# The feed-forward part of a batch as units between the next batch's score steps

## The chip, the cores and the metric

The kernel runs on one core of a Trainium2 chip. Its five engines work at the same time and wait for each other by semaphores: TensorE (PE) multiplies, VectorE (DVE) and ScalarE (ACT) work on tiles in SBUF and PSUM, GpSimd (POOL) works on tiles in SBUF, and SyncE (SP) issues most of the DMAs. The metric is the device time of one execution in microseconds.

## The reference

The input x is 4 batches of 1024 rows of 256 values. A memory of 77 rows per batch stands ahead of the keys. There are two blocks, each with a residual:

```
y  = x + attention(layernorm(x), mem)       16 heads of 16, causal behind the 77 memory rows, output projection and bias
out = y + ffn(layernorm(y))
ffn(v) = quant(gelu(quant(v) @ quant(w_fc).T + b_fc)) @ quant(w_proj).T + b_proj
```

`quant` gives each block of 32 values along a row one exponent, from the largest magnitude of the block, and rounds to 3 bits of mantissa. The hidden width is 1024, Gelu is the exact one.

## The kernel before, in words

A tile is 128 rows; there are 32 tiles, 8 in a batch. The heads are worked on in groups of four, so there are 16 head groups `kk`, four to a batch. A head group takes 14 steps of two half-steps (`half_step`, L662). In a half-step PE makes two pieces of score rows for the next group, from which DVE takes row maxima (`max_matmul` L400, `max_reduce` L423 and L425), and two pieces of transposed scores for this group (`score_matmul`, L463), which ACT turns into exponentials (`score_exp`, L474) and POOL masks (L479). `times_v` (L500) multiplies them with the values, two steps later. Row maxima go through DRAM back into a row of q (`put_max`, L436 and L437). After half of a group's steps `pack` copies the sums (L522) and sends them by DMA into `o_pk` and, the row sums, into DRAM.

PSUM has two buffers for the transposed scores (`ps_st`), three small ones that all else shares (`ps_s`, through `s_tile`), and one for the sums (`ps_av`).

The order of the work is written out: every engine runs its instructions in the order in which this program issues them (`manual_schedule`). `run` (L680) puts other work, called units, between half-steps. A unit is a function or a list of stages; `begin` runs the first at once and the others three half-steps apart (`LATER`), `tick` runs what is due. Before, the units of a head group are spread by their number. Units are the statistics and the normalization of the next batch (`stats_unit`, `norm_unit`), its projections (`v_unit`, `qk_unit`, `move_unit`), the quantized weights of the feed-forward part during batch 0 (`weight_unit`), the division by the row sums (`divide_unit`: a DMA in, a reciprocal on DVE L549, a DMA out, 16 broadcasting DMAs L557, two products on POOL L566) and the output projection with the first residual (`wout_unit`, L578 to L584).

All of x lies in SBUF from the start (`x_all`, loaded at L82); the residual is added into it. When attention is done for all batches, `inv_std` makes 32 inverse deviations at once, and a loop over the 32 tiles runs the feed-forward part with pools of its own: `in_unit` (normalize L781, quantize L188 to L201, transpose L788), `hid_unit` one tile behind it (matmuls L798 and L801, Gelu L806, quantize), `out_unit` two tiles behind (transpose L814, copy L816, matmuls L819 and L820, residual L822, output L823).

```
    for t in range(TT + 2):
        if t < TT:
            in_unit(t)
        if 1 <= t <= TT:
            hid_unit(t - 1)
        if t >= 2:
            out_unit(t - 2)
```

Of the kernel before, what the change touches and what calls it, by code (L numbers as in the profile page):

```python
# [17 lines left out]
P = 128  # L18
# [25 lines left out]
def kernel(  # L44
# [34 lines left out]
    x_all = const.tile([P, TT, D], F32, name="x_all")  # L79

    def load_x(t0, n):
        nc.sync.dma_start(  # L82
            out=x_all[:, t0 : t0 + n, :],
            in_=xf[t0 * P : (t0 + n) * P, :].rearrange("(t p) d -> p t d", p=P),
        )

    for t0 in range(0, NT, 2):
        load_x(t0, 2)
    ctx_sb = const.tile([M, B, D], F32, name="ctx_sb")
    nc.scalar.dma_start(out=ctx_sb, in_=mem.rearrange("b m d -> m b d"))  # L90
# [6 lines left out]
    for b in range(1, B):  # L97
        for half in range(2):
            load_x(b * NT + half * NT // 2, NT // 2)

# [58 lines left out]
    def stats(t, mv):  # L159
        st = small.tile([P, 6], F32, name="st")  # L160
        nc.vector.bn_stats(st, x_all[:, t, :])
        nc.vector.bn_aggr(mv[:, t, :], st)
# [18 lines left out]
    def block_quant(pool, src, n, dst):  # L181
# [4 lines left out]
        src3 = src.rearrange("p (n k) -> p n k", k=QBLK)  # L186
        amax = small.tile([P, nb], F32, name=f"amax{n}")
        nc.vector.tensor_reduce(amax, src3, axis=AX.X, op=ALU.max, apply_absolute_value=True)  # L188
        mag = small.tile([P, nb], F32, name=f"mag{n}")
# [7 lines left out]
        magb = mag.unsqueeze(2).broadcast_to([P, nb, QBLK])  # L197
        up = pool.tile([P, n], F32, name=f"up{n}")
        up3 = up.rearrange("p (n k) -> p n k", k=QBLK)
        nc.vector.tensor_tensor(up3, src3, magb, ALU.add)  # L200
        nc.gpsimd.tensor_tensor(  # L201
            dst.rearrange("p (n k) -> p n k", k=QBLK), up3, magb, ALU.subtract
# [9 lines left out]
    with ExitStack() as actx:  # L212
        ap = lambda name, bufs, **kw: actx.enter_context(tc.tile_pool(name=name, bufs=bufs, **kw))
        keep = ap("keep", 1)
        xtp = ap("xtp", 2)
        osp = ap("osp", 3)
        opp = ap("opp", 3)
        rbp = ap("rbp", 1)
        dram = ap("dram", 2, space=bass.MemoryType.DRAM)
        work = ap("work", 3)  # L220
        ptp = ap("ptp", 7)
        wst = ap("wst", 2)
# [17 lines left out]
        q_st = keep.tile([P, N], F32, name="q_st")  # L240
        k_st = keep.tile([P, KEYS], F32, name="k_st")
# [28 lines left out]
        normed = {b: 0 for b in range(B)}  # L270

        def stats_unit(b, half):
            def emit():
# [3 lines left out]
                if half == 1:  # L277
                    inv_std(mv1, rstd1, b * NT, (b + 1) * NT)
# [584 lines left out]
```

## Time and profile before

| | |
|---|---|
| time, median of 3 runs | 1213.57 us (1187.82 to 1215.45) |
| profiled execution | 1219.08 us, its span 1217.3 us |
| mean granted TensorE clock | 0.846 |
| busy: PE, DVE, ACT, POOL | 92%, 63%, 41%, 20% |
| tables loaded on ACT | 2 |
| last copy of attention sums (L522) | 981.1 us |

The profile is of one execution; the figures below come from it. A line of a group gives the source line, engine, operation, output and inputs with their shapes, the count, the busy time and the mean of one in ns, and then how long the engine stood before them and what ended that. A line of waits gives who waited for whom, the total in us, how often, and the longest. PE's busy time is modelled: a busy PE isn't PE at its peak. The clock line shows in tenths what clock the array was granted in each fortieth of the span.

### The profile page before, as it was taken

How to read it: one execution, taken by the hardware profiler on the slowest of the kernel's cores; microseconds unless marked ns; L12 is line 12 of the kernel's file. 1: busy time of each engine (PE TensorE's matmuls, PEld its weight loads, DVE VectorE, ACT ScalarE, POOL GpSimd, SP SyncE). 2: the span in 40 equal slices, each digit the busy share in tenths (PEclk: the TensorE clock that was granted, in tenths of full speed). 3: DMA queues.
4: the chain of work that ended last, by engine and by line, in shares of the span. 5: the costliest groups of instructions: out<-in, count | busy, mean ns of one | idle time of the engine just before them, and what ended most of it. 6: DMA issues, size and time to landing. Idle time of an engine off the chain costs nothing. (4 is left out here: it accounts for less than half of the span.)

```text
span 1217.3 us, 21139 instructions
## 1 busy us (share of the span) xinstructions
PE 1115.3 (92%) x8024; PEld 451.3 (37%) x8024; DVE 763.8 (63%) x2176; ACT 497.4 (41%) x708; POOL 247.1 (20%) x435
## 2 busy tenths in 40 slices
PE   3998999999979999997999999999999966888996
PEld 2433333433324334432343443434333232443333
DVE  7765765657557675665576665667772028997765
ACT  2123444534423555442435455444554302443333
POOL 3010211021111110112011110222111023445342
PEclk9976789979959999997799999999997565775557
DMA  7000001000110011003000100110000100000000
GB/s 218 22 20 15 19 20 35 24 19 21 38 49 2 12 26 25 8 8 76 11 6 16 40 3 12 44 44 7 6 12 7 25 25 0 31 23 22 22 18 27
DMA packets 31383, 32.17 MB, mean 26 GB/s; under 512 B 13364, under 2 KB 24942, under 8 KB 31281
## 3 DMA queue, kind: packets, MB, share of 16 engines
q1 hardware_dynamic: 29856, 29.43, 9.0%
q8 instruction: 63, 1.03, 0.4%
q10 hardware_dynamic: 1425, 1.38, 0.4%
q14 instruction: 39, 0.32, 0.1%
HBM read 12.39 MB, written 5.24 MB: 14 GB/s over the span
## 5 line engine op out<-in xcount | busy, mean ns | idle before, releaser
L474 ACT ACTIVATE pt<-st_ps 128x1024 f32<-128x1024 f32 (+4 forms) x448 | 354.1, 793 | 452.3 <-PE st_ps L463 236.3
L400 PE MATMUL s_ps<-kT,qT 32*128 32x205 f32 (+3 forms) x1736 | 498.2, 552 | 29.3 <-DVE mxp L425 19.2
L463 PE MATMUL st_ps<-qT,kT 32*128 32x512 f32 (+5 forms) x1792 | 513.1, 576 | 1.1 <-ACT pt L474 0.7
L425 DVE CUSTOM_DVE_ANT_0 junk<-s_ps,tri,mx 128x293 bf16<-128x293 f32 (+3 forms) x372 | 228.4, 614 | 91.6 <-PE s_ps L400 54.1
L400 PEld LDWEIGHTS s_ps<-kT,qT 32*128 32x128 f32 x1736 | 200.5, 195 | 210.6 <-issue 93.9
L479 POOL TENSOR_SCALAR_AFFINE_SELECT pt<-pt 128x254 f32<-128x254 f32 (+3 forms) x320 | 117.4, 367 | 772.0 <-ACT pt L474 772.0
L500 PE MATMUL av_ps<-pt,vaug 128*32 128x256 f32 (+7 forms) x3072 | 237.9, 384 | 6.0 <-POOL pt L479 3.6
L423 DVE TENSOR_REDUCE mx<-s_ps 128x1 f32<-128x296 f32 (+3 forms) x310 | 159.3, 554 | 97.6 <-PE s_ps L400 74.9
L463 PEld LDWEIGHTS st_ps<-qT,kT 32*128 32x128 f32 (+1 forms) x1792 | 199.3, 196 | 21.8 <-ACT pt L474 10.5
L500 PEld LDWEIGHTS av_ps<-pt,vaug 128*32 128x32 f32 (+1 forms) x3072 | 63.1, 112 | 267.6 <-issue 203.7
L425 DVE CUSTOM_DVE_ANT_0 junk<-s_ps,tri 128x205 bf16<-128x205 f32 (+2 forms) x186 | 94.2, 507 | 88.1 <-PE s_ps L400 62.4
L201 POOL TENSOR_TENSOR hq<-up,mag 128x1024 bf16<-128x1024 f32 x32 | 61.4, 1918 | 56.5 <-DVE up L200 50.5
L819 PE MATMUL y_ps<-wprT,hT 128*128 128x256 bf16 x256 | 51.1, 366 | 15.6 <-ACT hT L816 15.6
L798 PE MATMUL h_ps<-wfcT,xqT 128*128 128x512 bf16 x128 | 58.3, 536 | 2.8 <-ACT xqT L790 2.6
L578 PE MATMUL s_ps<-wo_sb,o_pk 128*128 128x256 f32 x128 | 42.0, 453 | 12.3 <-POOL o_pk L566 11.5
L806 ACT ACTIVATE h<-h_ps 128x1024 f32<-128x1024 f32 x32 | 32.8, 1025 | 48.3 <-PE h_ps L801 31.2
L549 DVE RECIPROCAL r<-sm 128x64 f32<-128x64 f32 x8 | 4.4, 550 | 76.6 <-DMA sm<-sums 76.6
L816 ACT COPY hT<-ht_ps 128x1024 bf16<-128x1024 bf16 x32 | 32.4, 1012 | 43.2 <-PE ht_ps L814 43.0
L188 DVE TENSOR_REDUCE amax<-h 128x32 f32<-128x1024 f32 x32 | 38.8, 1214 | 16.0 <-ACT h L806 15.9
L819 PEld LDWEIGHTS <-hT 128*128 128x128 bf16 x256 | 30.6, 127 | 32.6 <-ACT hT L816 19.2
L319 PE MATMUL s_ps<-wv,xT 128*128 128x256 f32 (+1 forms) x144 | 42.4, 419 | 0.1
L425 DVE DVE_READ_ACCUMULATOR2_ANT mxp<- 128x1 f32 x512 | 42.2, 82 | 0.0
(87 smaller groups left out, 783.9 us busy)
## 6 DMA issues: line engine op xcount, KB each, us to landing
kT<-k_st SPq DMA_DIRECT2D x16, 275.2 KB
qT<-q_st SPq DMA_DIRECT2D x16, 256.0 KB
o_pk<-o_st SPq DMA_DIRECT2D x32, 128.0 KB
rb<-rd SPq DMA_DIRECT2D x128, 32.0 KB
out_dram<-y_sb SPq DMA_DIRECT2D x32, 128.0 KB
x_all<-in_x_dram SPq DMA_DIRECT2D x6, 512.0 KB
x_all<-in_x_dram SPq DMA_DIRECT2D x4, 256.0 KB
sums<-o_st SPq DMA_DIRECT2D x64, 4.0 KB
```

The source lines that it names most:

```text
L201: nc.gpsimd.tensor_tensor(dst.rearrange("p (n k) -> p n k", k=QBLK), up3, magb, ALU.subtract)
L319: nc.tensor.matmul(vp[:nj, :], xT[b][:, k, jt * P : jt * P + nj], wv[:, k, :], start=(k == 0), stop=(k == KC - 1),)
L400: nc.tensor.matmul(sp[:, 0 : hi - lo], qTs[kk % NQK][rows, it * P : (it + 1) * P], kTs[kk % NQK][rows, lo:hi], start=True, stop=True,)
L423: nc.vector.tensor_reduce(into, sp[:, 0:w], axis=AX.X, op=ALU.max)
L425: nc.vector.tensor_tensor_reduce(junk[:, 0:w], sp[:, 0:w], mask, 1.0, before, ALU.add, ALU.max, into)
L463: nc.tensor.matmul(st[:nj, e, : i1 - i0], kTs[kk % NQK][rows, t * P : t * P + nj], qTs[kk % NQK][rows, i0:i1], start=True, stop=True,)
L474: nc.scalar.activation(pt[:nj, :, :w], st[:nj, :, :w], AF.Exp, scale=scale)
L479: nc.gpsimd.affine_select(out=pt[:nj, :, :behind], in_=pt[:nj, :, :behind], compare_op=ALU.is_ge, fill=0.0, base=base, pattern=[[0, 2], [1 ...
L500: nc.tensor.matmul(acc[c * PAD : (c + 1) * PAD, off + lo : off + hi], vaugs[b % 2][:nj, t, v0 : v0 + PAD], pts[kk, n, c // 2][:nj, c % 2, ...
L578: nc.tensor.matmul(yp, o_pk[b, it * P // ICW][:, k, it * P % ICW : it * P % ICW + P], wo_sb[:, k, :], start=(k == 0), stop=False,)
L798: nc.tensor.matmul(hp[:, cols], src[:, k, :], wfcT[:, k, cols], start=(k == 0), stop=False)
L819: nc.tensor.matmul(yp, hT[:, k, :], wprT[:, k, :], start=(k == 0), stop=False)
```

## The change

The loop at the end and its pools are gone. The feed-forward part is written as units like the others, and the units of batch b - 1 are put into the head groups of batch b. The last batch's run at the end.

- x is no longer held as a whole. Each batch's x is loaded into `xn` for its normalization, and each tile is loaded again into one of ten `x2` buffers when its residual is added (`wout_unit`), where it stays until it is written out.
- `divide_unit` issues its broadcasting DMAs two per half-step, its two products run on DVE and in two stages, the reciprocal comes four half-steps after the fetch, and both divisions of a batch begin as soon as the sums are there (`urgent`).
- The quantization is split: `quant_steps` finds the rounding constant, `quant_round` adds it in place on DVE and takes it off on POOL.
- `hidden_unit` takes four tiles at a time, in the buffers of the transposed scores, with Gelu on ACT; in the last batch one tile at a time.
- `out_unit` has four stages: `largest`, `rounding` one half-step later, `turn`, `project`.
- A unit has a cost in us and may have a condition (`ready`); `run` spreads units by cost.
- q and k share one staging tile `qk_st`; `pt` has 6 buffers for 7, `o_st` 2 for 3, `xT` 1 for 2, `xh` 4 for 3. The memory rows are loaded per batch.

```diff
...
         nc.vector.tensor_scalar(
             mag, mag, 1.5 * 2.0 ** -126, 2.0 ** (23 - MBITS), ALU.max, ALU.mult
         )
-        magb = mag.unsqueeze(2).broadcast_to([P, nb, QBLK])
+    def quant_round(src, mag, dst):
+        n = src.shape[-1]
+        magb = mag.unsqueeze(2).broadcast_to([P, n // QBLK, QBLK])
+        src3 = src.rearrange("p (n k) -> p n k", k=QBLK)
+        nc.vector.tensor_tensor(src3, src3, magb, ALU.add)
         nc.gpsimd.tensor_tensor(
-            dst.rearrange("p (n k) -> p n k", k=QBLK), up3, magb, ALU.subtract
+            dst.rearrange("p (n k) -> p n k", k=QBLK), src3, magb, ALU.subtract
         )
     mv1 = const.tile([P, TT, 2], F32, name="mv1")
...
-        xtp = ap("xtp", 2)
-        osp = ap("osp", 3)
+        xtp = ap("xtp", 1)
+        xnp = ap("xnp", 2)
+        osp = ap("osp", 2)
         opp = ap("opp", 3)
         rbp = ap("rbp", 1)
+        X2 = 10
+        xrp = ap("xrp", X2)
+        HBUF = 4
+        hp_ = ap("hp", HBUF)
+        ffn = ap("ffn", 2)
         dram = ap("dram", 2, space=bass.MemoryType.DRAM)
-        work = ap("work", 3)
-        ptp = ap("ptp", 7)
-        wst = ap("wst", 2)
+        work = ap("work", 4)
+        ptp = ap("ptp", 6)
         ps_st = ap("ps_st", 2, space=PSUM)
         ps_av = ap("ps_av", 1, space=PSUM)
         ps_s = ap("ps_s", 3, space=PSUM)
...
         mxps = [keep.tile([P, 2 * HPG * NT // 2], F32, name=f"mxp{i}") for i in range(2)]
         for i in range(2):
             nc.gpsimd.memset(mxps[i], 0.0)
...
-            def scale_sums():
-                o = o_pk[b, ic]
-                for k in range(KC):
-                    nc.gpsimd.tensor_tensor(o[:, k, :], o[:, k, :], got["rb"][:, k, :], ALU.mult)
-                divided.add((b, ic))
-            fetch.ready = lambda: sums_of.get((b, ic)) == NG
-            return [fetch, invert, spread, lambda: None, scale_sums]
+                got["rd"] = dram.tile([HEADS, ICW], F32, name="rd")
+                nc.sync.dma_start(out=got["rd"].rearrange("h (s j) -> (h s) j", s=SPH), in_=r)
+                got["rb"] = rbp.tile([P, KC, ICW], F32, name="rb")
+            def spread(h):
+                def emit():
+                    for i in range(h, h + 2):
+                        nc.sync.dma_start(
+                            out=got["rb"][i % HPC * HD : (i % HPC + 1) * HD, i // HPC, :],
+                            in_=got["rd"][i, :].partition_broadcast(HD),
+                        )
+                return emit
+            def scale_sums(k):
+                def emit():
+                    o = o_pk[b, ic][:, k, :]
+                    nc.vector.tensor_mul(o, o, got["rb"][:, k, :])
+                    if k == KC - 1:
+                        divided.add((b, ic))
+                        held["rb"] -= 1
+                return emit
+            fetch.ready = lambda: packed.get((b, ic)) == NG and not held["rb"]
+            stages = [fetch, (4, invert)]
+            stages += [(LATER if h == 0 else 1, spread(h)) for h in range(0, HEADS, 2)]
+            return cost(0.6, stages + [(4, scale_sums(0)), (1, scale_sums(1))])
...
         def wout_unit(b, it):
-            def emit():
-                t = b * NT + it
-                assert (b, it * P // ICW) in divided
+            t = b * NT + it
+            ic = it * P // ICW
+            def fetch():
+                x2[t] = xrp.tile([P, D], F32, name="x2")
+                nc.sync.dma_start(out=x2[t], in_=xf[t * P : (t + 1) * P, :])
...
+                nc.vector.tensor_add(x2[t], x2[t], yp)
+                stats(x2[t], mv2, t)
+                done["wout"] += 1
+            fetch.ready = lambda: (b, ic) in divided and len(x2) - done["out"] < X2
+            return cost(1.8, [fetch, project])
+        def wout_units(b, half):
+            return [wout_unit(b, half * HN + i) for i in range(HN)]
...
+        def root_unit(b, half):
+            def emit():
+                inv_std(mv2, rstd2, b * NT + half * HN, b * NT + (half + 1) * HN)
+                rooted.add(b * NT // HN + half)
+            emit.ready = lambda: done["wout"] >= b * NT + (half + 1) * HN
+            return cost(1.5, emit)
+        def in_unit(t):
+            got = {}
+            def quantize():
+                done["begun"] += 1
+                held["xq"] += 1
+                xh = work.tile([P, D], F32, name="xh")
+                nc.vector.tensor_scalar(
+                    xh, x2[t], mv2[:, t, 0:1], rstd2[:, t : t + 1], ALU.subtract, ALU.mult
+                )
+                got["xq"] = ffn.tile([P, D], BF16, name="xq", bufs=XQ)
+                quant_round(xh, quant_steps(xh, D, "x"), got["xq"])
+            def turn():
+                tp = s_tile([P, KC, P], BF16)
+                for k in range(KC):
+                    nc.tensor.transpose(tp[:, k, :], got["xq"][:, k * P : (k + 1) * P], identb)
+                held["xq"] -= 1
+                xqT[t] = ffn.tile([P, KC, P], BF16, name="xqT", bufs=HBUF + 1)
+                nc.scalar.copy(xqT[t], tp)
+            quantize.ready = lambda: (
+                t // HN in rooted and done["begun"] - len(hs) <= HBUF
+                and held["xq"] < XQ and held["xh"] < XH
+            )
+            return cost(1.6, [quantize, turn])
+        def hidden_unit(tiles):
+            def emit():
+                for t in tiles:
+                    hp = ps_st.tile([P, 2, ICW], F32, name="st_ps")
+                    for n in range(HID // ICW):
+                        for k in range(KC):
+                            nc.tensor.matmul(
+                                hp[:, n, :], xqT[t][:, k, :],
+                                wfcT[:, k, n * ICW : (n + 1) * ICW],
+                                start=(k == 0), stop=False,
+                            )
+                        nc.tensor.matmul(
+                            hp[:, n, :], ones3,
+                            bias3[:, B_FC + n * ICW : B_FC + (n + 1) * ICW],
+                            start=False, stop=True,
+                        )
+                    hs[t] = hp_.tile([P, HID], F32, name="h")
+                    nc.scalar.activation(
+                        hs[t], hp.rearrange("p e n -> p (e n)"), AF.Gelu
+                    )
+            emit.ready = lambda: (
+                all(t in xqT for t in tiles) and len(hs) + len(tiles) - done["round"] <= HBUF
+            )
+            return cost(1.4 * len(tiles), emit)
+        def out_unit(t):
+            got = {}
+            def largest():
+                held["hq"] += 1
+                got["mag"] = quant_steps(hs[t], HID, "h")
+            def rounding():
+                got["hq"] = ffn.tile([P, HID], BF16, name="hq")
+                quant_round(hs[t], got["mag"], got["hq"])
+                done["round"] += 1
+            def turn():
+                tp = s_tile([P, HC, P], BF16)
+                for k in range(HC):
+                    nc.tensor.transpose(tp[:, k, :], got["hq"][:, k * P : (k + 1) * P], identb)
+                held["hq"] -= 1
+                got["hT"] = ffn.tile([P, HC, P], BF16, name="hT")
+                nc.scalar.copy(got["hT"], tp)
+            def project():
+                yp = s_tile([P, D])
+                for k in range(HC):
+                    nc.tensor.matmul(
+                        yp, got["hT"][:, k, :], wprT[:, k, :], start=(k == 0), stop=False
+                    )
+                nc.tensor.matmul(yp, ones3, bias3[:, B_PROJ : B_PROJ + D], start=False, stop=True)
+                nc.vector.tensor_add(x2[t], x2[t], yp)
+                nc.sync.dma_start(out=of[t * P : (t + 1) * P, :], in_=x2[t])
+                done["out"] += 1
+            largest.ready = lambda: t in hs and held["hq"] < 2
+            return cost(4.4, [largest, (1, rounding), turn, project])
...
             stages[0]()
-            for i, stage in enumerate(stages[1:]):
-                pending.append((clock[0] + (i + 1) * LATER, stage))
+            at = clock[0]
+            for stage in stages[1:]:
+                delay, stage = stage if isinstance(stage, tuple) else (LATER, stage)
+                at += delay
+                pending.append((at, stage))
...
-                    share += len(extras) / spots
-                    while (
-                        todo
-                        and len(extras) - len(todo) < share - 1e-6
-                        and ready(todo[0])()
-                    ):
-                        begin(todo.popleft())
+                    share = min(share + rate, 2.5)
+                    if urgent and ready(urgent[0]):
+                        begin(urgent.pop(0))
+                    while todo and share > 0 and ready(todo[0]):
+                        u = todo.popleft()
+                        share -= price(u)
+                        begin(u)
...
+            if g == NG - 1:
+                urgent += [divide_unit(b, 0), divide_unit(b, 1)]
+            if f >= 0:
+                T = range(f * NT, (f + 1) * NT)
                 if g == 0:
-                    extras += batch_units(b + 1) + wouts
-                elif g >= 2:
-                    vs = v_units(b + 1)
-                    extras += vs[:5] if g == 2 else vs[5:]
+                    extras += loads + wout_units(f, 0) + qs + [root_unit(f, 0)]
+                    extras += merge(norms, wout_units(f, 1)) if norms else wout_units(f, 1)
+                    extras += [root_unit(f, 1)]
+                elif g == 1:
+                    extras += [in_unit(t) for t in T[:HN]] + [hidden_unit(T[:HN])]
+                    extras += [out_unit(T[0])] + [in_unit(t) for t in T[HN:]]
+                elif g == 2:
+                    extras += merge(vs[:5], [out_unit(t) for t in T[1:HN]]) + qs
+                    extras += [hidden_unit(T[HN:])]
+                else:
+                    extras += merge(vs[5:], [out_unit(t) for t in T[HN:]])
...
+        T = range((B - 1) * NT, B * NT)
+        todo = urgent + carry
+        chain = lambda ts: [f for t in ts for f in (in_unit(t), hidden_unit([t]), out_unit(t))]
+        todo += merge(chain(T[:HN]), wout_units(B - 1, 1)) + [root_unit(B - 1, 1)]
+        todo += chain(T[HN:])
+        while todo or pending:
             tick()
-        for u in end_units(B - 1):
-            u()
+            for u in list(todo):
+                if getattr(u[0] if isinstance(u, list) else u, "ready", lambda: True)():
+                    todo.remove(u)
+                    begin(u)
+                    break
     mode.close()
-    inv_std(mv2, rstd2, 0, TT)
...
```

## The prediction

> **What bounds the kernel now.** I read the page's busy times and clock first, then stretches by stage, then who waits for whom, then the costliest groups by shape.
>
> ```profile
> PE 1115.3 (92%) x8024; PEld 451.3 (37%) x8024; DVE 763.8 (63%) x2176; ACT 497.4 (41%) x708; POOL 247.1 (20%) x435
> ...
> PEclk9976789979959999997799999999997565775557
> ```
>
> ```profile
> 860.00:880.00 20.00, 20.00 (x204) 7.68 (x201) 15.04 (x45) 9.77 (x13) 3.66 (x10) 1.00 0.01 2
> ...
> 106.00:981.00 875.00, 847.43 (x6801) 330.28 (x6800) 521.93 (x1588) 395.75 (x565) 140.67 (x340) 0.91 0.09 22
> ...
> 981.00:1020.00 39.00, 20.70 (x57) 10.18 (x54) 19.47 (x72) 2.99 (x5) 5.82 (x7) 0.59 0.08 19
> 1020.00:1217.00 197.00, 168.00 (x788) 74.44 (x786) 147.71 (x288) 73.04 (x94) 85.31 (x60) 0.63 0.06 22
> ```
>
> The columns are busy us of PE, PEld, DVE, ACT and POOL, the granted clock, the DMA share, GB/s. There are two stages with different limits. To 981 us the score steps run: PE is named busy nearly throughout, but DVE is at 15.04 of 20 even in a clean stretch. From 981 on comes the tail: the last division and projections, then the feed-forward part (FFN) of all 32 tiles in 197 us, 6.2 us a tile, with half the TensorE clock granted for much of it. The tail is 236 us. So the question is what 24 of the 32 tiles cost when they are put between score steps.
>
> The copies of the attention sums (L522) start at 855.6 and 898.6 us in two consecutive head groups: 43.0 us for 28 half-steps without extras, 1.54 us each. In a half-step DVE reduces twice: the groups of L423 and L425 sum to 529 us over 448 half-steps, 1.18 us each. So about 0.35 us of slack per half-step, with only three PSUM buffers (`ps_s`) between the two engines. PE already waits for DVE's reductions:
>
> ```profile
> PEld s_ps L400 <- DVE mxp L425: 58.3, 92, 5.1
> ...
> PEld s_ps L400 <- DVE mx L423: 31.9, 71, 1.8
> ...
> PE s_ps L400 <- DVE mxp L425: 19.2, 11, 3.9
> ```
>
> What dense DVE work does to the clock is seen where batch 0 quantizes weights (stretches of 4 us, same columns):
>
> ```profile
> 244.00:248.00 4.00, 4.00 (x44) 1.39 (x41) 3.54 (x13) 1.49 (x3) 1.39 (x3) 1.00 0.11 33
> 248.00:252.00 4.00, 3.47 (x30) 1.36 (x26) 3.32 (x13) 0.94 (x3) 1.30 (x3) 0.84 0.12 37
> 252.00:256.00 4.00, 4.00 (x24) 1.44 (x26) 2.44 (x10) 0.67 (x2) 0.88 (x2) 0.50 0.00 0
> 256.00:260.00 4.00, 4.00 (x20) 1.78 (x20) 1.17 (x5) 1.42 (x2) 0.86 (x2) 0.50 0.00 0
> 260.00:264.00 4.00, 4.00 (x21) 1.50 (x20) 1.74 (x9) 2.01 (x3) 0.27 (x1) 0.50 0.00 0
> 264.00:268.00 4.00, 4.00 (x16) 1.65 (x17) 0.75 (x3) 0.93 (x3) 0.43 (x1) 0.52 0.04 6
> 268.00:272.00 4.00, 4.00 (x32) 1.61 (x34) 1.57 (x6) 2.50 (x5) 0.82 (x2) 1.00 0.12 40
> ```
>
> DVE is at 85 to 90% for some 12 us, PE gets gaps, and then the clock is 0.5 for 16 us with half as many matmuls per 4 us (20 instead of 42). I call that a dip.
>
> **What the Trainium skill says.** "TensorE: Matmul & The Clock Gate", section "Part 1: The HAM clock gate", says that the array's clock is either half or full, set by how busy the array was in a window of a few us. The trace agrees: windows read 0.50 or 1.00 and mixtures of both; its low stretches last 16 to 20 us. The same page, "Architectural detail", says DVE and ACT take instructions strictly in order. The trace agrees: the reciprocal L549 stood 34.6 us for its DMA and nothing of DVE passed it. "ScalarE: Activation LUTs", "What ACT_TABLE_LOAD costs", gives 1283 ns for a switch of tables; the trace has 1283 ns for both of its loads.
>
> **The change part by part.** Sums are against the profiled execution: 1219.1 us (span 1217.3), 5.5 above the median of 1213.6, which I take off at the end.
>
> (1) The tail loses 24 tiles. What is left after the last sums: in order of instructions, tiles 0 to 3 of batch 3 go first, beside the division's DMAs (before: 981 to 997), 4 x 6.2 = 25 us; then the scaling on DVE (1.2), four projections (5), the inverse root (2.9, like 1008.3 to 1011.4), and four tiles, 3 x 6.2 plus one tile's latency of about 21 (DVE 1.9, POOL 0.9, PE and copy 1, PE 2.6, Gelu 1.0, DVE 3.2, POOL 1.9, PE 2.3, copy 1.0, PE 2.2, DVE 0.4, output 2.5). That is 73 us, against 236: **-163**.
>
> (2) What a moved tile costs DVE comes from the rows of the FFN groups:
>
> ```profile
> L188 DVE TENSOR_REDUCE amax<-h 128x32 f32<-128x1024 f32 x32 | 38.8, 1214 | 16.0 <-ACT h L806 15.9
> ...
> L200 DVE TENSOR_TENSOR up<-h,mag 128x1024 f32<-128x1024 f32 x32 | 41.3, 1291 | 0.2
> ...
> L781 DVE TENSOR_SCALAR xh<-x_all,mv,rstd 128x256 f32<-128x256 f32 x32 | 17.5, 551 | 0.1
> ```
>
> in_unit: 551 (L781), 408 (L188), 248 + 217 (L190, L194), 472 (L200) = 1.90 us. out_unit: 1214 + 356 + 354 = 1.92 in one half-step, 1.29 in the next, and 0.42 for the residual. Sum 5.5 us a tile. Four tiles' out part falls into the last head group, where no reductions are left (DVE 0.55 us of 30 from 950 to 980) and costs DVE nothing: 24 x 5.53 - 4 x 3.63 = 118 us.
>
> PE: the FFN's matmul groups cover 168.0 us for 32 tiles at clock 0.63, 3.3 us a tile at full clock: 24 x 3.3 = 79 us.
>
> How much of these 197 us lengthens the path? Not none: a half-step with 1.9 us more on DVE has 3.1 us there against 1.54, and three buffers don't let PE run on. Followed through in order, 1.9 costs about 1.4 and 1.29 about 0.8; PE's matmuls come three half-steps after their DVE part, mostly on their own. The trace's nearest rows: six half-steps from 284.23 to 299.35 took 15.1 us, 5.9 over 6 x 1.54; one projection part took 1.98, so 3.9 to 4.0 remain for three weight quantizations (1.28 each on DVE) and two pairs of transposes (0.28), 4.4 in all: 0.9. Eight residual projections at full clock (L578, L584: 16.6 us of both engines) cost some 12.5 in the head groups around 800 us: 0.75. I take 0.8: **+158**; bounds 0.6 and 1.3 below.
>
> (3) Dips. in_unit comes four half-steps in a row, twice a batch, 4 x 3.1 us at DVE 95%: like 240 to 252. With the roots and statistics, three dips for each of two batches and two for the third are new. A dip of 16 us at half rate loses 7: **+56**. The bounds are no dip, and a clock that is low throughout.
>
> (4) Gelu in six bursts: 12 table loads, 1.28 each on ACT, which has work for 0.79 of 1.54 us. PE fills two `ps_st` buffers meanwhile; queued behind the loads are the next exponentials, which have two score buffers of lead. 1 us a burst, between 0 and 4: **+6**. The two scalings per division go from POOL (1274) to DVE; 12 halves at about 0.6 (L584's rate, twice its width), in half-steps of their own: **+5**.
>
> (5) Batch boundaries. The two intervals between such sums that hold a boundary are 75.3 and 61.1, then 68.2 and 61.7, then 54.0 and 53.8 us, against 43.0 plus extras of 15 or so. Reciprocal (6.7 and 5.7 us for its DMA on DVE), 16 `rb` DMAs in one block on SP (7.7), and `o_pk` waits of PE are in it. The change gives the reciprocal one more step, issues two DMAs per step, starts the first division a head group earlier and fetches before it projects: **-25**, between 0 and -38. 32 loads of x, and 16 of `xn` for 10 of `x_all`, come to SP's queue beside the row-maximum's two DMAs; at 0.6 us each (L599) and spread out, they are hidden by the half head group that these have; in one block they would cost what the `rb` block cost.
>
> (6) Start: only batch 0's x is loaded, but q's copy waits for k's move out of the one `qk_st`, and the root is made twice (4 us each): **+3**, between -3 and +8. SBUF that is made free has no price on the path.
>
> Sum: -163 + 158 + 56 + 6 + 5 - 25 + 3 = +40: 1259, less 5.5, about **1252 us**.
>
> **The rivals.** *The fill stays warm* (this one ends faster). DVE has 353 us free between 106 and 981, more than 118; if units overlap each other (one's PE part in another's DVE stall) the share is 0.6 and no dip is added: -163 + 118 + 6 + 5 - 25 + 3 = -56, 1158 us. For it: the eight projections near 800 us kept the clock at 1.00. Against: they weren't four in a row of 1.9. It decides if fewer than three or so dips are added at 0.8, or any number at 0.6.
> *Batch 0's rate.* The sums at 226.4 and 285.5 are 59.1 apart, 16.1 over clean; 7.4 for projections (9.3 of PE x 0.8) leave 8.7 for four weights of 1.64 on both engines: 1.3, dips in it. Then 197 x 1.3 = 256: -163 + 256 + 6 + 5 - 25 + 3 = +82, 1296 us; POOL's 1.9 us roundings, queued ahead of the masks (L479) and waiting for DVE in order, would add to it.
> *Units don't fit and slide into the tail*, 6.2 us a tile. In the changed order the eighth tile of batch 0 ends in the 25th step of its last head group, so I give it nothing.
>
> **How the numbers follow.** Forecast (1215 to 1280) 0.44; warm fill (1145 to 1200) 0.30; batch 0's rate (1280 to 1325) 0.18; between the first two, few dips, 0.08. 2% of 1213.6, about what can be told from no change, puts the limits at 1189 and 1238. Faster: most of the warm fill, 0.28. Slower: four fifths of the forecast and all of batch 0's rate, 0.53. Same: 0.19. The range leaves out the fast end of the warm fill and the slow end of batch 0's rate: 1165 to 1310. The likeliest case alone: 1215 to 1280.
>
> **What would show it.** The last sums copy later, near 1180, and a tail near 73 us; DVE over 80% from batch 1 on; PE's waits for reductions (110 us above) doubled; clock 0.5 in stretches after the rows of in_unit; 14 table loads. I am wrong if the clock stays at 1.00 in head groups 5 to 7, or if head groups grow by less than 10 us.

## The result, and the profile after

The changed kernel takes 1236.66 us (median of 4 runs, 1231.43 to 1238.72), the kernel before 1204.03 us beside it (4 runs). Over the fast runs alone, which leave out the two slow ones of before at 1213.57 and 1215.45 us, the ratio is 1.0375, 95% interval [1.0301, 1.0449]. It is slower by 3 to 4.5%. I had predicted 1252.

The execution of before whose profile the prediction uses, 1219.08 us, had a mean clock of 0.846; beside the later experiments before had about 0.87 and medians of 1196 to 1202 us, than which the changed kernel is 3% longer. Kernels made from before are compared with the runs of before beside them. Those made from the changed kernel are compared with its 1236.66 us, which was taken at another time, so differences of a few us mean little there.

The profiled execution took 1237.07 us. First its page, busy times and clock:

```profile
PE 1113.3 (90%) x8014; PEld 447.3 (36%) x8024; DVE 793.4 (64%) x2346; ACT 516.6 (42%) x720; POOL 226.0 (18%) x419
...
PEclk9778899999978689999979668999999796989665
```

Then its stretches of time, before and behind the last copy of sums (now L566, at 1134.95 us), and two of 20 us in batch 1; the columns are those of the prediction (busy us of PE, PEld, DVE, ACT, POOL, clock, DMA share, GB/s):

```profile
106.00:1134.95 1028.95, 976.14 (x7437) 383.41 (x7444) 661.26 (x1987) 472.99 (x652) 188.41 (x372) 0.90 0.10 27
1134.95:1235.30 100.35, 63.23 (x236) 27.23 (x240) 57.22 (x136) 20.61 (x26) 21.07 (x16) 0.60 0.10 29
400.00:420.00 20.00, 16.19 (x111) 6.76 (x107) 15.83 (x58) 5.03 (x13) 4.27 (x9) 0.75 0.02 4
420.00:440.00 20.00, 19.78 (x73) 4.58 (x72) 3.70 (x11) 10.60 (x13) 0.00 (x0) 0.50 0.03 9
```

The tail went from 236.2 to 100.4 us (-136), and the score steps grew from 981.1 to 1134.95 (+154). DVE is busy for 64% of the score steps, where it was 60% (521.93 of 875 us). Batch 1's in_units come in the third stretch (DVE 15.83 of 20), and behind them the clock is 0.50 for all of the fourth, as in the dips of the weights.

PE's waits for reductions, from the table of who waits for whom, make 169 us in these four lines:

```profile
PEld s_ps L444 <- DVE mxp L469: 85.1, 130, 5.2
...
PEld s_ps L444 <- DVE mx L467: 41.2, 63, 3.5
```

```profile
PE s_ps L444 <- DVE mxp L469: 28.8, 27, 4.5
...
PE s_ps L444 <- DVE mx L467: 14.0, 11, 2.8
```

Before they made 114.5: the three lines of the prediction and

```profile
PE s_ps L400 <- DVE mx L423: 5.1, 4, 1.3
```

### The profile page after: what moved, and what is told of

Same layout as the page of the kernel before. It is cut to its first block, busy times and chain, and to the rows that moved or that the text cites. A ratio compares the mean times of both kernels' runs of the same rounds, so it can differ in the third digit from the quotient of the medians.

```text
span 1235.3 us, 21300 instructions
## 1 busy us (share of the span) xinstructions
PE 1113.3 (90%) x8014; PEld 447.3 (36%) x8024; DVE 793.4 (64%) x2346; ACT 516.6 (42%) x720; POOL 226.0 (18%) x419
## 4 chain that ended last, share of the span: by engine, by line
PE 71%; DVE 18%; issue 3%; DMA 2%; ACT 2%; POOL 1%; SPq 1%; POOLq 0%; DVEq 0%; ACTq 0%
PE s_ps L444 24%; PE av_ps L544 14%; PE st_ps L507 12%; PE s_ps L387 5%; DVE junk L469 4%; PE st_ps L694 3%; PE s_ps L360 3%; PE s_ps L634 2%; PE s_ps L736 2%; PE st_ps L699 2%; DVE mx L467 2%; DVE amaxh L171 1%; DVE st L145 1%; PE s_ps L728 1%; ACT pt L518 1%
## 5 line engine op out<-in xcount | busy, mean ns | idle before, releaser
L444 PE MATMUL s_ps<-kT,qT 32*128 32x205 f32 (+3 forms) x1736 | 536.7, 570 | 53.9 <-DVE mxp L469 28.8
L507 PE MATMUL st_ps<-qT,kT 32*128 32x512 f32 (+5 forms) x1792 | 531.7, 575 | 1.0 <-DVE mx L469 0.6
L192 POOL TENSOR_TENSOR hq<-h,magh 128x1024 bf16<-128x1024 f32 x32 | 61.2, 1913 | 188.4 <-DVE h L191 159.1
L394 ACT COPY qk_st<-s_ps 128x512 f32<-128x512 f32 (+1 forms) x40 | 20.4, 514 | 78.3 <-PE s_ps L387 70.7
L694 PE MATMUL st_ps<-wfcT,xqT 128*128 128x512 bf16 x118 | 49.1, 501 | 4.2 <-ACT xqT L678 3.1
L705 ACT ACTIVATE h<-st_ps 128x1024 f32<-128x1024 f32 x32 | 32.8, 1024 | 44.4 <-PE st_ps L699 44.0
L731 ACT COPY hT<-s_ps 128x1024 bf16<-128x1024 bf16 x32 | 32.4, 1012 | 36.2 <-PE s_ps L728 35.7
L736 PE MATMUL s_ps<-wprT,hT 128*128 128x256 bf16 x256 | 42.2, 320 | 1.2 <-ACT hT L731 1.2
L387 PE MATMUL s_ps<-xT,wk_sb 128*128 128x512 f32 (+1 forms) x96 | 42.3, 575 | 0.4 <-ACT xT L348 0.4
L171 DVE TENSOR_REDUCE amaxh<-h 128x32 f32<-128x1024 f32 x32 | 38.6, 1207 | 5.7 <-ACT h L705 5.7
```

Source lines behind the costliest of these rows:

```text
L192: nc.gpsimd.tensor_tensor(dst.rearrange("p (n k) -> p n k", k=QBLK), src3, magb, ALU.subtract)
L387: nc.tensor.matmul(pp[:, :n], w[:, k, hi * P : (hi + 1) * P], xT[b][:, k, first + lo : first + lo + n], start=(k == 0), stop=(k == KC - 1),)
L444: nc.tensor.matmul(sp[:, 0 : hi - lo], qTs[kk % NQK][rows, it * P : (it + 1) * P], kTs[kk % NQK][rows, lo:hi], start=True, stop=True,)
L507: nc.tensor.matmul(st[:nj, e, : i1 - i0], kTs[kk % NQK][rows, t * P : t * P + nj], qTs[kk % NQK][rows, i0:i1], start=True, stop=True,)
L694: nc.tensor.matmul(hp[:, n, :], xqT[t][:, k, :], wfcT[:, k, n * ICW : (n + 1) * ICW], start=(k == 0), stop=False,)
L736: nc.tensor.matmul(yp, got["hT"][:, k, :], wprT[:, k, :], start=(k == 0), stop=False)
```

## The experiments

For the clock I use one more figure: half-clock time, the time that the array spent at a granted clock of 0.50, which is the sum over stretches of 2 x (1 - clock) x their length. From 300 us to the last copy it is 119 us in the profile of before and 178 in the changed kernel.

Each kernel has one profile, and these differ from run to run: in the kernels made from the changed one, the first copy of batch 1 comes at 343.0 to 349.0 us, though none has run a moved tile by then. So I measure the score steps from that copy to the last one:

| kernel made from the changed one | from the first copy of batch 1 to the last copy, us | half-clock time in it, us |
|---|---|---|
| changed | 785.9 | 174 |
| without the 24 tiles | 642.9 | 117 |
| h not rounded | 759.7 | 171 |
| fewer matmuls | 787.8 | 250 |
| matmuls twice | 808.1 | 143 |
| in_units apart | 769.5 | 130 |
| h's addition on POOL | 785.1 | 198 |
| Gelu tile by tile | 793.0 | 178 |

**What the 24 tiles cost in either place.** Two kernels leave the feed-forward part of batches 0 to 2 out and write y instead of it; one is made from the changed kernel, one from the kernel before.

```diff
-                    extras += [in_unit(t) for t in T[:HN]] + [hidden_unit(T[:HN])]
-                    extras += [out_unit(T[0])] + [in_unit(t) for t in T[HN:]]
+                    pass
...
-                    extras += merge(vs[:5], [out_unit(t) for t in T[1:HN]]) + qs
-                    extras += [hidden_unit(T[HN:])]
+                    extras += vs[:5] + qs
...
-                    extras += merge(vs[5:], [out_unit(t) for t in T[HN:]])
+                    extras += vs[5:]
```

> Leaves out the feed-forward units of batches 0 to 2 (in, hidden, out); the first residual of these batches is written out as the result, and batch 3 is as in the changed kernel. It measures what 24 tiles cost between score steps: the changed kernel's last copy of the attention sums lies at 1135 us. By the prediction's sizes (0.8 of 197 us, 56 for dips of the clock, 6 for Gelu) it comes at 1135 - 220 = 915 us. If units hide well and something else in the change made the score steps longer (loads of x on SP's queue, smaller pools, divisions on DVE), it stays above 1010. With no units, DVE busy falls under 75% of any stretch and the stretches at clock 0.5 after 360 us go.

```diff
-    for t in range(TT + 2):
...
+    for t in range(T0, TT + 2):      (T0 is TT - NT)
```

> The kernel before with the feed-forward part of batches 0 to 2 left out of its last loop: x with the first residual is written out for these, eight tiles remain. Set against the changed kernel without its units (1090.8 us, last copy of sums 990 us) it measures what all else in the change costs. If the rest of the change helps (25 us at the batch boundaries, as predicted), this takes 1090 + 25 = 1115 us or more. If the rest of the change costs time in the score steps (the profiles give 990 against 981 for the last copy, and that profile of before had a low clock, 0.846 against 0.87 in later runs), it takes 1196 - 24 x 6.2 = about 1048 us, its last copy near 960.

Measured: 1090.82 us (before beside it 1196.53) and 1057.12 us (before 1198.85). The last copy comes at 990.1 us in the first, between the 915 and the 1010 of its expectation. So in the tail of before 24 tiles cost 1198.85 - 1057.12 = 141.7 us, 5.9 each; between score steps they cost 1236.66 - 1090.82 = 145.8, 6.1 each. Moving them gains nothing. The rest of the change costs 1090.82 - 1057.12 = 33.7 us, and 145.8 - 141.7 + 33.7 = 37.8 is the whole difference.

The times at which the first half of a head group's sums is copied tell where. The table has the first group of each batch, and the last copy of all (us):

| | batch 0 | batch 1 | batch 2 | batch 3 | last |
|---|---|---|---|---|---|
| before without the tiles | 108.1 | 350.4 | 576.6 | 787.0 | 967.7 |
| changed, without the tiles | 114.9 | 347.2 | 579.3 | 805.4 | 990.1 |
| changed | 116.1 | 349.0 | 636.8 | 923.2 | 1134.95 |

From row two to row three, batch 0's and 1's eight tiles add 56 and 60 us, over 7 us a tile, but batch 2's only 27. Those end in the last head group, which has no row maxima: its last half takes 22 us there, against 34.5 without the tiles; the clock was 1.00 in the one and 0.50 in the other.

From row one to row two there are +6.8 at the start and +15.6 later; the tail grows by a further 12 (88.6 to 100.3). DVE's work after 300 us grows by 26 us: two scalings per division (9.6), and inverse roots, of which each of the two normalizations now makes one for every half batch; before, the first made one per batch and the second one for all at the end. Of the root's lines, this one (kernel without tiles, from the changed one, 300 to 990 us) comes 30 times, in ten roots:

```profile
L612 DVE TENSOR_TENSOR o_pk<-o_pk,rb 128x512 f32<-128x512 f32 x14 | 9.6, 687 | 9.9 <-DMA rb<-rd 9.8 <-issue 0.2
...
L162 DVE TENSOR_SCALAR e<-e 128x4 f32<-128x4 f32 x30 | 5.3, 177 | 1.0
```

and its counterpart (without tiles, from before, 300 to 968 us) 6 times, in two:

```profile
L178 DVE TENSOR_SCALAR e<-e 128x8 f32<-128x8 f32 x6 | 1.0, 171 | 0.2
```

**DVE's share: no rounding of h.** The largest values and the rounding of h are left out (POOL takes off zero): 3.2 us less of DVE a tile.

```diff
-                got["mag"] = quant_steps(hs[t], HID, "h")
...
-                quant_round(hs[t], got["mag"], got["hq"])
+                nc.gpsimd.tensor_tensor(
+                    got["hq"].rearrange("p (n k) -> p n k", k=QBLK),
+                    hs[t].rearrange("p (n k) -> p n k", k=QBLK),
+                    nomag.unsqueeze(2).broadcast_to([P, HID // QBLK, QBLK]), ALU.subtract
+                )
```

> Leaves out the rounding of h on DVE (largest magnitude, two small steps, the addition: 3.2 us a tile); POOL subtracts zero, so its work, the transposes and all matmuls stay. If DVE's queue is what the units lengthen: 20 tiles x 3.2 x 0.7 is 45 us off the score steps, last copy of sums near 1090, and some 15 us off the tail: about 1175 us in all. If PE's matmuls or the clock after the in_units carry the loss: last copy above 1120, in all above 1215.

Measured: 1183.09 us, 53.6 less. The last copy is at 1102.7, 32 earlier, but 6 of these come before the first tile. By the table the score steps are 26 us shorter, with nearly the same half-clock time. Four tiles' out parts lie in the last head group, which has no reductions to delay; the other 20 tiles have 20 x 3.2 = 64 us less of DVE, so its share of the path is 26 of 64, 0.41. The tail is 23 us shorter, for eight tiles less of rounding and for a half-clock time that fell from 81 to 42 us; these two aren't told apart.

**PE's share: fewer matmuls, and more.** One kernel leaves out four of six matmuls of the hidden layer and seven of eight of the projection (some 39 us of PE in 24 tiles). The other does those over k twice; the second pass starts the sums anew, so the results are the same.

```diff
-                        for k in range(KC):
...
-                            hp[:, n, :], ones3,
-                            bias3[:, B_FC + n * ICW : B_FC + (n + 1) * ICW],
-                            start=False, stop=True,
+                            hp[:, n, :], xqT[t][:, 0, :],
+                            wfcT[:, 0, n * ICW : (n + 1) * ICW],
+                            start=True, stop=True,
...
-                for k in range(HC):
+                for k in range(1):
```

> Leaves out matmuls of the feed-forward part: hidden has one of two k and no bias (2 of 6 matmuls of 512 columns), project 1 of 8 k and the bias. At full clock that is some 1.6 us of PE a tile, 39 us for 24 tiles; DVE, POOL and ACT work stays. If PE's added work lies on the path: last copy of sums at 1135 - 32 = 1103 or less. If DVE's queue sets the half-steps and PE's part hides in them: above 1122. The tail loses up to 20 us either way.

```diff
-                        for k in range(KC):
+                        for k, end in [*((k, k == KC - 1) for k in range(KC)), *((k, False) for k in range(KC))]:
...
-                                start=(k == 0), stop=False,
+                                start=(k == 0), stop=end,
...
-                for k in range(HC):
+                for k, end in [*((k, k == HC - 1) for k in range(HC)), *((k, False) for k in range(HC))]:
```

> hidden and project run their matmuls twice (the second pass starts anew, same results): four of 512 columns and eight of 256 more a tile, some 1.7 us of PE at full clock, 41 us for 24 tiles. With fewer matmuls the last copy stayed at 1136 us while stretches at half clock after 300 us grew from 178 to 256 us. If denser PE work keeps the clock up, they shrink below 140 us and the last copy moves by under 15 us. If PE's work just adds: last copy 1135 + 33 or later, low stretches as before. The tail, at half clock, gets up to 25 us longer either way.

Measured: 1216.08 us with fewer (1209 to 1223), but the last copy stood where it was (1136.2), and half-clock time from 300 us on rose from 178 to 256. With more, 1261.74, the last copy 22 us later, and half-clock time fell to 150. Fewer matmuls came out as the expectation has it for work that hides in DVE's, more matmuls as neither of its cases. One reading fits both: PE's work has a price on the path, but thin work lets the clock fall and dense work holds it up. How large the price is then depends on what half clock costs, for which the next kernel gives a figure.

**The dips: in_units apart.** They begin at least three half-steps apart, the second four a head group later.

```diff
+                and (t >= TT - NT or clock[0] - done["at"] >= 3)
...
-                    extras += [out_unit(T[0])] + [in_unit(t) for t in T[HN:]]
+                    extras += [out_unit(T[0])]
...
-                    extras += merge(vs[:5], [out_unit(t) for t in T[1:HN]]) + qs
+                    extras += merge(
+                        vs[:5], [out_unit(t) for t in T[1:HN]], [in_unit(t) for t in T[HN:]]
+                    ) + qs
```

> Same work, other order: in_units come at least three half-steps apart instead of four in a row, and the second four move from the second to the third head group. If rows of in_units make the clock fall (dips of 16 us, 7 us each, six of them): last copy of sums near 1095, in all about 1195, and the stretches at 0.5 in 400 to 440, 690 to 750 and 1010 to 1040 us go. If only the amount of DVE work counts: 1237 within 10 us.

Measured: 1225.41 us, ratio to before 1.0252 [1.0202, 1.0301]; 11 less than the changed kernel, so the order does count, by a quarter of what was expected. By the table the score steps are 16 us shorter with 44 us less of half clock: 0.37 for each us. This rests on one profile of each kernel, and the edit takes DVE's work apart as well, so the clock alone may be worth less. The tiles add 56 us of half clock to the kernel without them, at that rate 21 us.

At this rate the two kernels before it give PE's share. With more matmuls the score steps are 22 us longer in spite of 31 us less of half clock: 22 + 31 x 0.37 = 33 for 41 us of PE, 0.8. With fewer they are 2 us longer with 76 us more: 28 - 2 = 26 for 39, 0.7.

**h's rounding on POOL, and Gelu tile by tile.**

```diff
-        nc.vector.tensor_tensor(src3, src3, magb, ALU.add)
+        add.tensor_tensor(src3, src3, magb, ALU.add)
...
-                quant_round(hs[t], got["mag"], got["hq"])
+                quant_round(
+                    hs[t], got["mag"], got["hq"], nc.gpsimd if t < TT - NT else nc.vector
+                )
```

> The addition that rounds h goes from DVE to POOL for the 24 tiles between score steps: 1.29 us a tile off DVE, 1.9 us a tile onto POOL, in front of the masks. Same results. If DVE's queue sets the length at the rate that leaving the rounding out showed (32 us for 64 us of DVE): 20 x 1.29 x 0.5 = 13 us less, about 1223. If POOL's order in front of the masks makes PE wait: 1240 or more, and PE's waits for POOL's masks grow beyond 33 us.

```diff
-                    extras += [in_unit(t) for t in T[:HN]] + [hidden_unit(T[:HN])]
+                    extras += [in_unit(t) for t in T[:HN]] + [hidden_unit([t]) for t in T[:HN]]
```

> Gelu one tile at a time between score steps instead of four: 50 table loads instead of 14, 36 x 1.28 = 46 us more on ACT. By the prediction's 1 us a burst: 18 more bursts, 1237 + 18 = 1255, bounds 1237 (hidden: ACT is busy for half of a half-step) and 1290 (each load on the path).

Measured: 1233.01 us (1219.8 to 1233.7), 4 less than the changed kernel. That is neither of the two cases, and too little to tell from no change; half-clock time rose by 24 us, which at 0.37 would hide 9. Gelu by single tiles: 1245.03 us (two runs), 8.4 more for 36 more table loads, which hold ACT for 46 us. A load then costs some 0.2 us, the bursts' 12 about 3.

**Tiles in the last head group.** Batch 2's cheap tiles point there. These two kernels are the kernel before with tiles 0 to 3, or 0 to 7, run in the last head group, in buffers that are free by then.

```diff
+        at_spot = {0: [lambda: inv_std(mv2, rstd2, 0, EARLY)]}
+        for j in range(0, EARLY, 4):
+            ts = range(j, min(j + 4, EARLY))
+            first = 1 + j // 4 * 12
+            for i, t in enumerate(ts):
+                at_spot.setdefault(first + 2 * i, []).append(early_in(t))
+            at_spot.setdefault(first + 10, []).append(lambda ts=ts: burst(ts))
+            for i, t in enumerate(ts):
+                at_spot.setdefault(first + 11 + 2 * i, []).append(early_out(t))
```

> The kernel before, with the feed-forward part of tiles 0 to 3 alone put into the last head group (batch 3, group 3), where no row maxima are left: DVE has 0.55 us of work in 30, PE is named busy throughout at clock 0.50, and the last half of this group takes 35 us, against 22 in the changed kernel, whose four last out parts lie there. Theory A (what makes a tile dear between score steps is DVE's share and the clock, so the last group takes tiles for nothing, and the added matmuls raise its clock): 4 x 5.9 = 24 us less of tail, the last half some 12 us shorter, 4 us for one more inverse root: some 30 us under before, last copy of sums 10 us earlier. Theory B (a tile costs about 6 us wherever it is put, as the 24 tiles did in both kernels): within 8 us of before, last copy 16 us or more later.

> As the kernel with four early tiles, but with tiles 0 to 7: four more are begun in the second half of the last head group, and their out parts fall behind it, beside the last division's DMAs, where before has DVE at 19.5 and PE at 20.7 of 39 us. Theory A: 47 us less of tail, last half 10 us shorter or so, 4 us for the root and some 8 for what doesn't fit: 40 to 50 us under before. Theory B: within 10 us of before.

Measured: 1184.09 us with four, ratio 0.9893 [0.9812, 0.9975], and 1183.79 with eight, 0.9877 [0.9736, 1.0017]. Four make it faster, by about half of what theory A expected, and the next four bring nothing that shows. With four the last group takes 67.9 us (54.8 in the profile of before), which takes back a part of what the tail gains. I take a group from the copy that ends the group ahead of it to its own last copy. In it PE is named busy, and the clock is low for some 48 us of the 67.9:

```profile
912.70:980.60 67.90, 65.36 (x385) 21.86 (x385) 19.34 (x36) 31.25 (x42) 19.09 (x28) 0.64 0.08 22
```

**Matmuls for nobody.** In the kernel before, each half-step of the last head group gets two matmuls over the whole array that nobody reads.

```diff
+                    if kk == B * NG - 1:
+                        idle = s_tile([P, ICW])
+                        for i in range(2):
+                            nc.tensor.matmul(
+                                idle, wprT[:, 0, 0:P], wfcT[:, 0, 0:ICW], start=True, stop=True
+                            )
```

> The kernel before, with two more matmuls of 128x128 by 128x512 in each of the 28 half-steps of the last head group; nobody reads them. 56 matmuls, some 12 us of PE at full clock. It tells whether dense work on the whole array raises the clock of this stretch. Theory A (it does): clock from 0.50 to 0.9 or more, the last half group 25 us or less for 35, the last copy up to 10 us earlier in spite of the added work. Theory B (the clock stays): 12 to 24 us later.

Measured: 1189.1 us (13 runs), ratio 0.9901 [0.9854, 0.9948]: work for nobody makes it 1% faster. The last group in before and then with the filling:

```profile
926.30:981.10 54.80, 52.77 (x285) 16.27 (x285) 0.55 (x1) 19.05 (x27) 8.74 (x19) 0.50 0.07 17
```

```profile
915.20:959.70 44.50, 44.00 (x337) 13.43 (x334) 0.55 (x1) 19.25 (x28) 8.74 (x19) 1.00 0.07 21
```

There are 52 more matmuls in the records, the same work on the other engines, and 10.3 us less. The profile of before isn't an odd one here: in the two kernels without tiles, whose last group isn't filled either, it takes 54.6 and 53.7 us at clock 0.51.

**Both, and the tail kept dense.** Four tiles in the last head group (their root in half-step 3), the two unread matmuls in its half-steps, and more of them where PE stood in the tail.

```diff
+        fill(56)
         for u in end_units(B - 1):
             u()
+        fill(40)
...
         yp = ps_y.tile([P, D], F32, name="y_ps")
+        for i in range(6):
+            nc.tensor.matmul(
+                yp, wprT[:, 0, 0:P], wfcT[:, 0, 0:D], start=True, stop=True
+            )
```

> The two things that made the kernel before faster, together: tiles 0 to 3 in the last head group (their inverse root three half-steps later than in the kernel with four early tiles, where the group entered at clock 0.50 behind it) with the two unread matmuls in each of its half-steps. To these, unread matmuls where PE has nothing: 56 while the last division is awaited, 40 beside the last inverse root, and six of 256 columns per tile in the last loop, ahead of the output matmuls that wait for the copy of hT (12.0 us of PE's waits in the loop of before, 11 times). If dense matmuls keep the clock up, the last head group takes about 50 us with its four tiles (67.9 without the filling, 54.8 in before, 44.5 with the filling alone), and the loop runs at DVE's 5.2 us a tile for 6.2: 10 + 24 + up to 25 us, 1145 to 1165. If the clock of the loop is set by something else, the filling there costs up to 0.7 us a tile: 1175 to 1190.

Measured: 1152.92 us (6 runs, 1151.4 to 1174.3), ratio to before 0.9654 [0.9591, 0.9717]. It beats both kernels; which of its parts gains how much was not tried singly. Stretches of its trace, the last head group and the loop:

```profile
912.60:970.20 57.60, 56.32 (x430) 20.59 (x434) 17.97 (x32) 31.09 (x41) 18.66 (x27) 1.00 0.09 23
...
1040.00:1140.00 100.00, 88.17 (x637) 48.15 (x646) 92.30 (x195) 48.51 (x62) 60.03 (x40) 1.00 0.08 29
```

and two of the loop of before:

```profile
1040.00:1100.00 60.00, 50.33 (x289) 24.42 (x288) 56.62 (x107) 27.64 (x34) 29.97 (x21) 0.80 0.08 29
1100.00:1180.00 80.00, 72.35 (x292) 30.49 (x292) 55.12 (x115) 25.98 (x34) 34.77 (x24) 0.50 0.05 19
```

The clock is 1.00 for all of both, where before had 0.50 for 80 us. The group with its four tiles took 57.6 us for 67.9; its root also comes three half-steps later. From one copy of hT to the next the loop took 4.71 us a tile, for 5.67 in before (first to last, 28 and 32 tiles). The nearer comparison is the kernel with four early tiles and no filling, whose loop has the same 28 tiles. It took 5.19 us a tile, and the same stretch reads

```profile
1040.00:1140.00 100.00, 81.67 (x458) 39.55 (x457) 91.86 (x172) 40.94 (x51) 50.67 (x35) 0.76 0.07 26
```

So the filling of the loop is worth about 0.5 us a tile, 13 us in all, and not the 27 that the profile of before suggests.

## Why the prediction was right, point by point

Slower was right, and so was the size, within 16 us; but the size is luck. The sum of (1) to (6) was +40 us, and 38 were measured (1236.66 - 1198.85), with parts that are wrong by more than this total: the tiles between score steps were put 74 us too dear, and against them the tail stands with 33 us too cheap and the rest of the change in the score steps with 39. What is left of the miss is the base: 1213.6 us there, 1198.85 beside the later runs. (The sum as written, 1259 less 5.5, gives 1253.5 and not 1252.)

**The failed step is the rest of the change, (5) and (6) with the scalings of (4): -25 + 3 + 5 = -17 predicted, +34 measured** by the two kernels without the tiles, +22 of it in the score steps and 12 in the tail. The start grew by 6.8 us for 3. Of the 25 us that (5) promised little is seen. The prediction counts two intervals to a boundary: the first of each shrank by 9.3, 9.7 and 1.5 us, but the second grew by 3.1, 4.9 and 5.3, so that together they are 7 us shorter. The intervals from the second to the third group of batches 1 and 2 grew by 10.1 us each, and there it is work that was moved: in the first of them the traces have 40 matmuls of projections for 16.

What the sum had no term for is what the finer roots and divisions add: 26 us of DVE's work in the score steps, eight more roots among it. I had costed "the root is made twice" at the start alone. As an estimate from the rates measured above, 26 us of DVE at 0.41 and 16 us more of half clock after 300 us (105 to 120) at 0.37 are 17 us, about the 15.6 by which the score steps behind the start grew. No run took the roots or the divisions out singly, so this division stays open.

**(2) to (4), the tiles between score steps: 158 + 56 + 6 = 220 predicted, 146 measured.** The share of 0.8 was near for PE (0.7 to 0.8) and double of what DVE's turned out to be (0.41). So 118 x 0.41 + 79 x 0.75 = 107 in place of 158. Dips: eight of 16 us, 128 us at half clock for 56 us of time, were forecast; 56 us of half clock were added, some 21 us of time. Gelu: 3 in place of 6. That makes 131; 12 of the 143 us in the table stay unexplained. The dips were where I put them; that the dense matmuls behind the thin stretches hold the clock up elsewhere, and so leave fewer in net, fits the two kernels with fewer and more matmuls but wasn't tried by itself. And the prediction reads the low stretches of before as 16 to 20 us long: its trace has them from 7 to 89 us.

**(1) The tail: -163 predicted, -136 measured** in the traces, -130 by the runs beside each other (-141.7 for the tiles and the 12 above). 100.4 us are left, not 73. The last batch's first four projections and their root, for which I had no time behind the last copy, fill the stretch to 1148 us; and the fourth in_unit runs at 1166.63, with the second division's scaling behind it at 1169.45:

```profile
1166.63 0.41 DVE L666 TENSOR_SCALAR xh<-x,mv,rstd 128x256 f32<-128x256 f32 x1
...
1169.45 1.71 DVE L612 TENSOR_TENSOR o_pk<-o_pk,rb 128x512 f32<-128x512 f32 x2
```

Units begin in the order of the list, one per half-step, and DVE does that scaling behind the fourth in_unit, so the second four tiles start late. The clock of this tail is 0.60.

**The signs.** Right: a tail and score steps that move against each other, the clock at 0.50 behind the rows of in_unit, 14 table loads. Wrong: last copy near 1180 (1135), a tail near 73 (100.4), DVE over 80% (64%), waits doubled (1.5 times). The warm fill named a share of 0.6 without dips; the share came near it (107 of 197), and the dips were there. Batch 0's rate, 1.3, did not come.

## What to carry to other kernels

Filling an engine's gaps gains only if the stage that is filled has room in the engine that sets its pace. Here the same tile cost 7 us between score steps with row maxima, 6 in a loop of its own and 3.4 where half of its batch fell in a group without them. Price the bookkeeping of the finer pieces as well (a root per half batch, scalings per half), since it comes as often as they do. And before moving work, read the granted clock of the stage that it is to leave: here the loop at the end ran at 0.63. Four tiles in the one group that had room, with unread matmuls there and in the tail, took 3.5% off before, where moving 24 tiles gained nothing.

## What the runs showed of the hardware that was not expected

A PE that is named busy can stay at half clock. The Trainium skill, "TensorE: Matmul & The Clock Gate", section "Part 1: The HAM clock gate", gives full clock after one busy window of some 3.4 us; in the last head group of before PE was named busy for 52.77 of 54.80 us, and the clock was 0.50 throughout. With two matmuls over the whole array in each half-step it was 1.00 throughout. Here the measurement decides: what the profile names busy isn't enough.

In before and in the two kernels without tiles the clock was 1.00 until the last group and fell within 1.5 us of its start. In the filled kernels it stayed at 1.00; their unread matmuls begin a few us ahead of that point (909.26 us, with the group taken from 915.16). So the filling was seen to hold a full clock. Dense work was also seen to raise a low one: in the kernel with four early tiles and no filling the clock was 0.50 from 914.7 us and 1.00 from 962.5, as the first output matmuls of these tiles ran.

Score matmuls use 32 of the array's rows each. That can't be all, since the prediction's stretch from 860 to 880 us has more of them in each us than the last group, among 204 matmuls in 20 us, and is at 1.00. Whether it is the number of matmuls, their mixture or short gaps that counts, no run tells apart.

Removing matmuls can therefore gain nothing in the score steps: 39 us less of PE's work left the end of the score steps where it was and made half-clock time 78 us longer.
